# A fixed instruction order for the first batch's entry into a quantised attention and LoRA kernel

## The chip, the core and the metric

The kernel runs on one core of a Trainium2 chip. A core has a matrix engine (TensorE, "PE" in the profile, with its weight loads as "PEld"), a vector engine (VectorE, "DVE"), a scalar engine (ScalarE, "ACT"), a general engine (GpSimd, "POOL") and a queue engine (SyncE, "SP") that here only issues DMA transfers. Each engine executes its own instructions in the order in which they stand in its queue, and waits for the others by semaphores. The metric is the device time of one execution in microseconds (us), smaller being better.

## What is computed

Both layers work on two batches of 1024 tokens with 2048 features. The first is a product of two fake-quantised matrices, the second a feed-forward product with low-rank additions:

```python
def fake_quant(x, scale, zp):
    q = jnp.clip(jnp.round(x / s + z), 0.0, 255.0)
    return (q - z) * s

x = x + matmul(fake_quant(layernorm(x)), fake_quant(ctx))     # ctx: 2 x 2048 x 2048
h = layernorm(x)
x = x + (matmul(h, kernel) + bias                              # kernel: 2048 x 2048
         + low-rank terms of lora_A, lora_B chosen by gate, and of the shared pair)
```

`setup_inputs` gives x, ctx, four quantisation parameters, the gate (8 groups by 16 adapters), the kernel, the bias and the LoRA matrices, all float32.

## The kernel before

**Staging.** The two batches run one after the other. For each, the attention product comes first, then the normalisation for the second layer, then the feed-forward product as a seven-product scheme in two levels (`OUTER`, `INNER`, function `product`), in which TensorE is occupied nearly without a gap. During the last of the outer steps of the first batch, the second batch's ctx blocks and token tiles are already prepared. For the first batch nothing runs ahead, and the start of the program is this batch's entry.

**Tokens.** A batch has 8 token tiles of 128, in four groups of two. `prep_x` prepares one tile. VectorE takes statistics (`bn_stats`, four of 512 columns, L283; `norm_stats`, with the square root on ScalarE, L261), and seven small operations give scale and offset. ScalarE writes the quantised tile as uint8 (L295) and then, in two halves, as bf16 with 128 subtracted and with the row sum (L298). TensorE transposes each half in eight pieces of 128 (L303), and VectorE copies them out of PSUM (L304). `r_s` is the tile's row sum times a constant (L308). The uint8 halves and the bf16 halves of all tiles share the buffer `wk`.

**Context.** ctx is taken in four column blocks of 512, each in eight row blocks of 256 rows (512 KB). The ten buffers `lit` take the loads in turn. `quantise` turns one into bf16: ScalarE scales and clips at 0 into int16 (L314), VectorE clips at 255 and subtracts 128 (L317). Three buffers `q2b` stand between. `column_term` sums a finished block's columns: 16 small matmuls into four partial sums (L333), a copy (L343), an f32 matmul (L345) and a scaling on VectorE (L348).

**A pair.** `xattn_pair(b, n, g)` multiplies column block n with token group g: for both tiles ScalarE writes column term plus row sum into PSUM (L359), TensorE adds 16 matmuls (L361), then VectorE adds the result to `y` (L370) and takes statistics of it (L372). `ps_acc` has three accumulators for the pairs, used in turn; the small PSUM pool `ps_m` has two buffers for transposes and column sums.

**What sets the order.** The program is written for a scheduler that sorts each engine's instructions when the program is built: what was written earlier goes first when it is ready by the scheduler's own estimate, and what is ready may pass what is not. `tc.high_priority()` puts the writes of L359 ahead. `tc.issue_after(opened.ins)` puts VectorE's part of the tiles 4 to 7 behind the first pair's sum. The loads all go through SP's queue: token tile 0, two ctx blocks, tile 1, seven ctx blocks, tiles 2 and 3, then one ctx block for each one that is quantised, and tiles 4 to 7 behind the last quantisation of column block 0. `ahead[0]` limits how many loads are out at a time.

The order in which the first batch's entry is written is at the end of the function, at `for b in range(B)`: tile 0, eight quantisations with tile 1 among them, the column term, pair (0, 0), four quantisations, tiles 2 and 3, pair (0, 1), four quantisations, the second column term, pairs (1, 0) and (1, 1), and then the tiles and pairs of groups 2 and 3. Early in the program stand the gate values (L236 to L248): masks from the identity, a gate transfer on ScalarE's queue, products and sums on VectorE, and for each batch the matrix `gmat` (L694), which the LoRA steps use.

Of the kernel before, what the change touches and what calls it, by code (L numbers as in the profile page):

```python
# [10 lines left out]
F32 = mybir.dt.float32  # L11
# [55 lines left out]
def tile_quant_xattn_then_lora_ffn(  # L67
# [119 lines left out]


# [4 lines left out]
    ahead[0] = 2  # L193
    load_next()
    load_x(0, 1)
    ahead[0] = 9
    load_next()
    load_x(0, 2)
    load_x(0, 3)
# [11 lines left out]
    nc.gpsimd.memset(n_centre, -CENTRE)  # L211
    nc.vector.tensor_mul(s12, s1, s2)
# [16 lines left out]
    for tag in ("acc0", "acc1", "delta"):  # L229
# [3 lines left out]


    m_ad = const.tile([P, NL], F32, tag="m_ad", name="m_ad")
    nc.vector.tensor_reduce(m_ad, ident.rearrange("p (n r) -> p n r", r=RC), AX.X, ALU.add)  # L236
    m_rk = const.tile([P, RC], F32, tag="m_rk", name="m_rk")
    nc.vector.tensor_reduce(m_rk, ident.rearrange("p (n r) -> p r n", r=RC), AX.X, ALU.add)
    gate_b = const.tile([P, GB, NL], F32, tag="gate_b", name="gate_b")
    nc.scalar.dma_start(  # L240
        out=gate_b.rearrange("p b n -> p (b n)"),
        in_=gate.rearrange("b n -> (b n)").partition_broadcast(P),
    )
    gval = const.tile([P, GB], F32, tag="gval", name="gval")
    nc.vector.tensor_tensor(gate_b, gate_b, m_ad.unsqueeze(1).to_broadcast([P, GB, NL]), ALU.mult)
    for b in range(B):
        for i in range(2):
            nc.vector.tensor_reduce(  # L248
                gval[:, ds(b * GPB + i * 2, 2)], gate_b[:, b * GPB + i : (b + 1) * GPB : 2, :], AX.X, ALU.add
            )  # L250

    def norm_stats(stats, name):

        mv = small.tile([P, 2], F32, tag="mv", name=f"mv_{name}")
# [4 lines left out]
        nc.scalar.activation(sd, ve, AF.Sqrt)  # L261
        r0 = small.tile([P, 1], F32, tag="r0", name=f"r0_{name}")
# [14 lines left out]
    def prep_x(b, m, c1T, wk):  # L277

        nm = f"{b}_{m}"
# [4 lines left out]
        mean, rstd = norm_stats(st1[:, m], f"a{nm}")  # L284
# [5 lines left out]
        nc.vector.tensor_sub(o, z1, o)  # L290

# [3 lines left out]
        nc.scalar.activation(q8, ym, AF.Identity, bias=o, scale=k)  # L295
        rsum = small.tile([P, 2], F32, tag="rsum", name=f"rsum_{nm}")
        for h in range(2):
            nc.scalar.activation(  # L298
                qh[:, ds(h * H, H)], q8[:, ds(h * H, H)], AF.Identity, bias=n_centre, accum_out=rsum[:, h : h + 1]
            )  # L300
            pt = ps_m.tile([P, KH, P], BF16, tag="pm", name=f"pt_{nm}_{h}")
# [6 lines left out]
        nc.vector.tensor_mul(r_s[:, m : m + 1], r_c, d2)  # L308

    def quantise(c2, r):  # L310

        buf, t = next_loaded()
        qi = q2b.take()
        nc.scalar.activation(qi, t, AF.Relu, bias=z2, scale=inv2)  # L314
# [595 lines left out]
```

## Time and profile before

| what | value |
|---|---|
| time, median of 3 runs | 1128.51 us (1127.28 to 1128.93) |
| time of the profiled execution | 1128.61 us |
| span of the profile | 1126.8 us |
| TensorE busy | 1072.4 us (95%) |
| VectorE, ScalarE, GpSimd busy | 741.5, 261.1, 266.6 us |
| first attention matmul starts | 42.31 us |
| first matmul of the fifth pair starts | 83.87 us |

The profile is of one execution. "Busy" counts the time in which an engine executes something; a matmul's end is modelled, and matmuls overlap their weight loads. In the 40 slices each digit is the busy share of 28 us in tenths. A line of the timeline gives start, duration, engine, source line, operation, tiles and shapes; in brackets stands how long the engine was idle just before and what ended that.

### The profile page before, as it was taken

To read this page: it belongs to the slowest core of one execution; us is meant where nothing else is said; L and a number is where in the kernel's file an instruction comes from. 1 tells how busy PE (TensorE), PEld (TensorE's weight loads), DVE (VectorE), ACT (ScalarE), POOL (GpSimd) and SP (SyncE) were. 2 spreads that over 40 slices of the span, in tenths; PEclk is the share of its full clock that TensorE was granted. 3 is DMA by queue.
4 is the path that set the end of the run, shared out by engine and by line. 5 is a ranking of instruction groups with operands and counts; after the bars stand their busy time and mean duration, and the time that the engine had idled before them with its cause. 6 is when DMAs were issued, how large, how long until landed. Compare 5 with 4: busy or idle time off the path is not lost.

```text
span 1126.8 us, 10619 instructions
## 1 busy us (share of the span) xinstructions
PE 1072.4 (95%) x3926; PEld 489.3 (43%) x3926; DVE 741.5 (66%) x969; ACT 261.1 (23%) x342; POOL 266.6 (24%) x106
## 2 busy tenths in 40 slices
PE   1689899999999999999999999999999999999998
PEld 0244334554444444444444433455444444444443
DVE  4685547576696768568777654766668586865861
ACT  5875513320001010001375761232000000000000
POOL 0000000234253422525000000022535343243600
PEclk9999999999999999999999999999999999999999
DMA  8991935885789757489857094588668875749611
GB/s 307 391 244 35 282 124 217 298 322 205 246 285 377 266 181 264 141 301 355 285 184 228 1 277 154 182 301 314 244 215 293 295 255 181 256 145 322 213 38 56
DMA packets 120772, 261.35 MB, mean 232 GB/s; under 512 B 11920, under 2 KB 16144, under 8 KB 119568
## 3 DMA queue, kind: packets, MB, share of 16 engines
q1 hardware_dynamic: 99264, 218.65, 56.6%
q10 hardware_dynamic: 21456, 42.02, 10.5%
q8 instruction: 31, 0.51, 0.2%
q14 instruction: 21, 0.17, 0.0%
HBM read 224.99 MB, written 37.75 MB: 233 GB/s over the span
## 4 chain that ended last, share of the span: by engine, by line
PE 80%; DMA 7%; DVE 6%; ACT 4%; issue 1%; SPq 1%; ACTq 0%; DVEq 0%
PE fu L611 33%; PE fv L611 17%; PE pa L361 13%; PE fw L611 9%; DMA lit<-in_ctx_dram 4%; PE pl L483 3%; PE ptz L432 2%; DVE big L560 1%; PE pg_a L383 1%; DVE st L283 1%; PE pg_b L383 1%; ACT big L298 1%; ACT big L295 1%; DMA bd<-q2b 1%; DMA big<-in_w_dram 1%
## 5 line engine op out<-in xcount | busy, mean ns | idle before, releaser
L611 PE MATMUL fu<-big,lit 128*128 128x512 f32 x896 | 396.3, 594 | 2.4 <-DVE y L629 2.4
L560 POOL TENSOR_TENSOR lit<-lit,lit 128x1024 f32<-128x1024 f32 x56 | 165.2, 2957 | 539.4 <-PE pa L361 209.1
L611 PEld LDWEIGHTS fu<-big,lit 128*128 128x128 f32 x896 | 167.8, 190 | 208.2 <-issue 206.7
L361 PE MATMUL pa<-big,big 128*128 128x512 bf16 x1024 | 238.0, 382 | 11.9 <-ACT pa L359 10.6
L611 PE MATMUL fv<-big,lit 128*128 128x512 f32 x448 | 198.1, 594 | 0.0
L551 POOL TENSOR_TENSOR lit<-lit,lit 128x1024 f32<-128x1024 f32 x40 | 100.9, 2524 | 283.4 <-DMA lit<-zs 255.5
L560 DVE TENSOR_TENSOR big<-big,big 128x2048 f32<-128x2048 f32 x56 | 159.4, 2850 | 5.9 <-PE ptz L432 5.3
L361 PEld LDWEIGHTS <-big 128*128 128x128 bf16 x1024 | 97.0, 98 | 146.5 <-issue 44.3
L629 DVE TENSOR_TENSOR y<-y,fu 128x1024 f32<-128x1024 f32 (+1 forms) x98 | 113.7, 1194 | 67.2 <-PE fu L611 66.8
L611 PEld LDWEIGHTS fv<-big,lit 128*128 128x128 f32 x448 | 84.3, 190 | 105.0 <-issue 105.0
L629 DVE TENSOR_TENSOR y<-y,fv 128x1024 f32<-128x1024 f32 x48 | 56.8, 1218 | 91.1 <-PE fv L611 91.1
L478 ACT COPY pl<-bias 128x1024 f32<-128x1024 f32 x32 | 32.6, 1017 | 344.9 <-DVE y L493 327.1
L314 ACT ACTIVATE q2b<-lit,sc,inv 128x1024 int16<-128x1024 f32 x64 | 76.6, 1230 | 146.4 <-DMA lit<-in_ctx_dram 124.7
L551 DVE TENSOR_TENSOR big<-big,big 128x2048 f32<-128x2048 f32 x40 | 101.7, 2544 | 13.2 <-DMA big<-in_w_dram 13.2
L611 PE MATMUL fw<-big,lit 128*128 128x512 f32 x224 | 100.6, 596 | 0.1
L370 DVE SCALAR_TENSOR_TENSOR y<-pa,k_s,y 128x1024 f32<-128x1024 f32 x32 | 41.0, 1282 | 69.7 <-PE pa L361 69.7
L359 ACT ACTIVATE pa<-bp,r_s 128x512 f32<-128x512 f32 x64 | 42.8, 684 | 105.6 <-PE pa L361 60.5
L629 DVE TENSOR_TENSOR y<-y,fw 128x1024 f32<-128x1024 f32 x24 | 28.4, 1217 | 52.5 <-PE fw L611 52.5
L611 PEld LDWEIGHTS fw<-big,lit 128*128 128x128 f32 x224 | 41.3, 190 | 48.7 <-issue 48.2
L303 PE MATMUL pt<-ident_h,big 128*128 128x128 bf16 x256 | 20.3, 231 | 29.6 <-ACT big L298 29.4
L283 DVE BATCH_NORM_STATS2 st<-y 128x6 f32<-128x512 f32 x64 | 42.1, 680 | 2.9 <-DMA y<-in_x_dram 2.9
L317 DVE TENSOR_SCALAR big<-q2b 128x1024 bf16<-128x1024 int16 x64 | 27.6, 440 | 23.7 <-ACT q2b L314 20.5
(79 smaller groups left out, 609.9 us busy)
## 6 DMA issues: line engine op xcount, KB each, us to landing
big<-in_w_dram SPq DMA_DIRECT2D x96, 1024.0 KB
lit<-zs SPq DMA_DIRECT2D x88, 512.0 KB
lit<-in_ctx_dram SPq DMA_DIRECT2D x64, 512.0 KB
out_dram<-y ACTq DMA_DIRECT2D x30, 512.0 KB
zs<-lit ACTq DMA_DIRECT2D x24, 512.0 KB
y<-in_x_dram SPq DMA_DIRECT2D x8, 1024.0 KB
lit<-in_lora_a_dram SPq DMA_DIRECT2D x32, 256.0 KB
lit<-in_lora_bt_dram SPq DMA_DIRECT2D x32, 256.0 KB
```

The lines of the kernel that those rows point to most:

```text
L283: nc.vector.bn_stats(st1[:, m, n, :], ym[:, ds(n * NB, NB)])
L314: nc.scalar.activation(qi, t, AF.Relu, bias=z2, scale=inv2)
L317: nc.vector.tensor_scalar(c2[r // 4][:, ds(2 * (r % 4), 2), :], qi, QMAX, CENTRE, ALU.min, ALU.subtract)
L359: nc.scalar.activation(pa[:, j, :], colt[n], AF.Identity, bias=r_s[:, m : m + 1])
L361: nc.tensor.matmul(pa[:, j, :], c1T[g][:, k, ds(j * P, P)], c2[k // 8][:, k % 8, :], start=False, stop=(k == KT - 1), skip_group_check=True,)
L370: summed = nc.vector.scalar_tensor_tensor(yp, pa, s12, yp, ALU.mult, ALU.add)
L478: nc.scalar.copy(pl, self.bb.unsqueeze(1).to_broadcast([P, 2, NB]))
L483: nc.tensor.matmul(pl[:, i, ds(h * (NB // 2), NB // 2)], axT[rows, pr, ds(j * P, P)], self.bp[rows, ds(h * (NB // 2), NB // 2)], start=Fal ...
L551: line(eng.tensor_tensor(got[0], got[0], got[1], ALU.add if terms[1][2] > 0 else ALU.subtract))
L560: line(eng.tensor_tensor(out_t, at[p], at[q], op))
L611: nc.tensor.matmul(ps[:, m, :], at[:, k, ds(m * P, P)], bt[:, k, :], start=(opens and k == 0), stop=(ends and k == KQ - 1), skip_group_che ...
L629: line(nc.vector.tensor_tensor(yp, yp, chains[chain][:, js, :], ALU.add if sign > 0 else ALU.subtract))
```

## The change

The entry of the first batch, up to and with pair (0, 1), is written as one function, `begin_first`, and a context manager `in_order` ties every instruction of VectorE, ScalarE, TensorE and SyncE in it to the one before it on the same engine, so that the scheduler keeps the written order on these engines. To be able to interleave them, `prep_x`, `quantise` and `xattn_pair` become generators of steps. Each `next` runs one step and `fin` runs what is left. A tile's steps are: statistics and square root; the seven small operations; the uint8 tile; bf16 half 0; half 1; transposes and copy of half 0; of half 1; row sum.

In this order the second pair is (1, 0), the third (0, 1). All of column block 1 is loaded and quantised ahead of token tile 2, whose load stands behind 16 ctx blocks. Five of the sixteen quantisations (rows 1, 3, 7 of block 0, rows 2, 4 of block 1) use `quantise_v`, both steps on VectorE with a uint8 between. For these two blocks the column term is 16 whole matmuls into one PSUM buffer (`column_sum`), without the copy and the f32 matmul. Twelve matmuls on constants (`keep_busy`) stand among them. A square root of a constant is computed at the program's start. The gate values and their transfer move to the end of the entry, ahead of the second half of pair (0, 1). Four ctx blocks instead of two are loaded ahead of tile 1, and the limit of loads becomes 10.

```diff
+    last_of = {}
+    @contextmanager
+    def in_order(*engines):
+        traced = nc.cur_bb.bb.instructions
+        last = traced[-1]
+        yield
+        start = next(k for k in reversed(range(len(traced))) if traced[k] is last) + 1
+        for i in list(traced[start:]):
+            if i.engine in engines:
+                if i.engine in last_of:
+                    tc.add_manual_dep(
+                        i,
+                        last_of[i.engine].name,
+                        mybir.DependencyInfo(mybir.DependencyClass.NoSync, mybir.DependencyReason.DATA),
+                        reason="in_order",
+                    )
+                last_of[i.engine] = i
...
     load_x(0, 0)
-    ahead[0] = 2
+    ahead[0] = 4
     load_next()
     load_x(0, 1)
-    ahead[0] = 9
+    ahead[0] = 8
     load_next()
-    load_x(0, 2)
-    load_x(0, 3)
+    ahead[0] = 10
+    load_next()
...
+    warm = const.tile([P, 1], F32, tag="warm", name="warm")
+    nc.gpsimd.memset(warm, 1.0)
+    nc.scalar.activation(warm, warm, AF.Sqrt)
...
-    m_ad = const.tile([P, NL], F32, tag="m_ad", name="m_ad")
...
+    def gate_values():
+        m_ad = const.tile([P, NL], F32, tag="m_ad", name="m_ad")
+        nc.vector.tensor_reduce(m_ad, ident.rearrange("p (n r) -> p n r", r=RC), AX.X, ALU.add)
+        nc.vector.tensor_reduce(m_rk, ident.rearrange("p (n r) -> p r n", r=RC), AX.X, ALU.add)
+        gate_b = const.tile([P, GB, NL], F32, tag="gate_b", name="gate_b")
+        nc.scalar.dma_start(
+            out=gate_b.rearrange("p b n -> p (b n)"),
+            in_=gate.rearrange("b n -> (b n)").partition_broadcast(P),
+        )
...
+    def begin_stats(stats, name):
         mv = small.tile([P, 2], F32, tag="mv", name=f"mv_{name}")
         nc.vector.bn_aggr(mv, stats.rearrange("p n s -> p (n s)"))
         ve = small.tile([P, 1], F32, tag="ve", name=f"ve_{name}")
         nc.vector.tensor_scalar_add(ve, mv[:, 1:2], EPS)
         sd = small.tile([P, 1], F32, tag="sd", name=f"sd_{name}")
         nc.scalar.activation(sd, ve, AF.Sqrt)
+        return mv, ve, sd, name
+    def end_stats(mv, ve, sd, name):
...
+    def prep_x_steps(b, m, c1T, wk):
...
-        mean, rstd = norm_stats(st1[:, m], f"a{nm}")
+        begun = begin_stats(st1[:, m], f"a{nm}")
+        yield
+        mean, rstd = end_stats(*begun)
...
         nc.scalar.activation(q8, ym, AF.Identity, bias=o, scale=k)
+        yield
         rsum = small.tile([P, 2], F32, tag="rsum", name=f"rsum_{nm}")
         for h in range(2):
             nc.scalar.activation(
                 qh[:, ds(h * H, H)], q8[:, ds(h * H, H)], AF.Identity, bias=n_centre, accum_out=rsum[:, h : h + 1]
             )
+            yield
+        for h in range(2):
             pt = ps_m.tile([P, KH, P], BF16, tag="pm", name=f"pt_{nm}_{h}")
             for kt in range(KH):
                 nc.tensor.transpose(pt[:, kt, :], qh[:, ds(h * H + kt * P, P)], ident_h)
             nc.vector.tensor_copy(c1T[g][:, ds(h * KH, KH), tok], pt)
+            yield
...
+    def quantise_steps(c2, r):
         buf, t = next_loaded()
         qi = q2b.take()
         nc.scalar.activation(qi, t, AF.Relu, bias=z2, scale=inv2)
         lit.give(buf)
         load_next()
+        yield
         nc.vector.tensor_scalar(c2[r // 4][:, ds(2 * (r % 4), 2), :], qi, QMAX, CENTRE, ALU.min, ALU.subtract)
+        q2b.give(qi)
+    def quantise_v(c2, r):
+        buf, t = next_loaded()
+        qi = q2b.take()
+        q8 = flat(qi)[:, 0:NB].bitcast(U8).rearrange("p (k n) -> p k n", k=2)
+        nc.vector.tensor_scalar(q8, t, inv2, z2, ALU.mult, ALU.add)
+        lit.give(buf)
+        load_next()
+        nc.vector.tensor_scalar(c2[r // 4][:, ds(2 * (r % 4), 2), :], q8, CENTRE, None, ALU.subtract)
         q2b.give(qi)
...
+    def column_sum(pc, c2, ks):
+        for k in ks:
+            nc.tensor.matmul(pc, ones_h, c2[k // 8][:, k % 8, :], start=(k == 0), stop=(k == KT - 1))
+    def column_end(pc, n):
...
+    def xattn_steps(b, n, g, c1T, c2, apart=False):
         cols = ds(n * NB, NB)
         pairs.append((b, n, g))
         pa = ps_acc.tile([P, MG, NB], F32, tag=("acc0", "acc1", "delta")[len(pairs) % 3], name=f"pa_{b}_{n}_{g}")
-        for j in range(MG):
+        def first(j):
             m = g * MG + j
             with tc.high_priority():
                 nc.scalar.activation(pa[:, j, :], colt[n], AF.Identity, bias=r_s[:, m : m + 1])
+        if not apart:
+            for j in range(MG):
+                first(j)
+        for j in range(MG):
+            if apart:
+                first(j)
+            yield
             for k in range(KT):
+                if k == KT // 2:
+                    yield
...
+    def begin_first():
+        X = [prep_x_steps(0, m, c1T, wk) for m in range(4)]
+        def fin(gen):
+            for _ in gen:
+                pass
+        def q(n, r):
+            gen = quantise_steps(c2[n], r)
+            next(gen)
+            return gen
+        def keep_busy(n):
+            for i in range(n):
+                nc.tensor.matmul(idle[:, i % 2, :], ones_h, ones_h[:, 0:1].to_broadcast([P, NB]), start=True, stop=True)
+        idle = ps_acc.tile([P, 2, NB], F32, tag="delta", name="idle")
+        q0 = q(0, 0)
+        next(X[0])
+        fin(q0)
+        next(X[0])
+        quantise_v(c2[0], 1)
+        q2 = q(0, 2)
+        next(X[0])
+        fin(q2)
+        quantise_v(c2[0], 3)
+        next(X[0])
+        next(X[0])
+        pc = ps_m.tile([P, NB], F32, tag="pm", name="pc_first")
+        column_sum(pc, c2[0], range(8))
+        q4 = q(0, 4)
+        next(X[1])
+        q5 = q(0, 5)
+        load_x(0, 2)
+        load_x(0, 3)
+        next(X[1])
+        next(X[0])
+        fin(X[0])
+        keep_busy(8)
+        q6 = q(0, 6)
+        fin(q4)
+        fin(q5)
+        column_sum(pc, c2[0], range(8, 12))
+        keep_busy(4)
+        next(X[1])
+        quantise_v(c2[0], 7)
+        load_x(0, 4)
+        load_x(0, 5)
+        fin(q6)
+        column_sum(pc, c2[0], range(12, 16))
+        next(X[1])
+        column_end(pc, 0)
+        A = xattn_steps(0, 0, 0, c1T, c2[0], apart=True)
+        next(A)
+        next(X[1])
+        next(X[1])
+        next(A)
+        p0 = q(1, 0)
+        p1 = q(1, 1)
+        fin(p0)
+        fin(X[1])
+        next(A)
+        next(A)
+        quantise_v(c2[1], 2)
+        p3 = q(1, 3)
+        load_x(0, 6)
+        load_x(0, 7)
+        fin(p1)
+        quantise_v(c2[1], 4)
+        p5 = q(1, 5)
+        pc = ps_m.tile([P, NB], F32, tag="pm", name="pc_second")
+        next(A)
+        column_sum(pc, c2[1], range(0, 6))
+        next(X[2])
+        fin(p3)
+        p6 = q(1, 6)
+        fin(p5)
+        p7 = q(1, 7)
+        next(A)
+        fin(p6)
+        fin(p7)
+        column_sum(pc, c2[1], range(6, 16))
+        column_end(pc, 1)
+        next(X[2])
+        next(X[2])
+        A2 = xattn_steps(0, 1, 0, c1T, c2[1])
+        next(A2)
+        next(X[3])
+        next(X[2])
+        next(X[2])
+        next(X[3])
+        next(A2)
+        next(A2)
+        next(X[2])
+        fin(X[2])
+        next(A2)
+        next(A2)
+        fin(A)
+        next(X[3])
+        A3 = xattn_steps(0, 0, 1, c1T, c2[0], apart=True)
+        next(A3)
+        next(X[3])
+        next(X[3])
+        next(A2)
+        next(A3)
+        next(A3)
+        fin(A2)
+        next(X[3])
+        fin(X[3])
+        gate_values()
+        gate_matrix(0)
+        next(A3)
+        fin(A3)
+    def gate_matrix(b):
...
+    for b in range(B):
+        if b > 0:
+            gate_matrix(b)
         if b == 0:
             open_c2(0)
-            prep_x(0, 0, c1T, wk)
-            for r in range(NR):
-                quantise(c2[0], r)
-                if r == 3:
-                    prep_x(0, 1, c1T, wk)
-            for m in range(4, MT):
-                load_x(0, m)
             open_c2(1)
-            column_term(b, 0, c2[0])
-        opened = xattn_pair(b, 0, 0, c1T, c2[0])
-        if b == 0:
-            for r in range(4):
-                quantise(c2[1], r)
-            for m in (2, 3):
-                prep_x(b, m, c1T, wk)
-        xattn_pair(b, 0, 1, c1T, c2[0])
-        if b == 0:
-            for r in range(4, NR):
-                quantise(c2[1], r)
-            column_term(b, 1, c2[1])
-        for g in range(2):
-            xattn_pair(b, 1, g, c1T, c2[1])
+            with in_order(
+                mybir.EngineType.DVE, mybir.EngineType.Activation, mybir.EngineType.PE, mybir.EngineType.SP
+            ):
+                begin_first()
+            opened = summed[0]
+            xattn_pair(b, 1, 1, c1T, c2[1])
+        else:
+            opened = xattn_pair(b, 0, 0, c1T, c2[0])
+            xattn_pair(b, 0, 1, c1T, c2[0])
+            for g in range(2):
+                xattn_pair(b, 1, g, c1T, c2[1])
```

## The prediction

> **What bounds the kernel now.** I read the engine shares first, then the forty slices, then windows around the entry, then the timeline of the entry engine by engine.
>
> ```profile
> PE 1072.4 (95%) x3926; PEld 489.3 (43%) x3926; DVE 741.5 (66%) x969; ACT 261.1 (23%) x342; POOL 266.6 (24%) x106
> ...
> PE   1689899999999999999999999999999999999998
> ```
>
> TensorE (PE) is busy 95%, and what it lacks, 54.4 us, lies mostly in the first two slices of 28 us. The windows split it:
>
> ```profile
> 0.00:42.30 42.30, 10.77 (x56) 4.90 (x57) 22.34 (x71) 24.95 (x28) 1.25 (x10) 1.00 0.89 336
> 42.30:83.87 41.57, 35.79 (x203) 16.83 (x203) 30.16 (x97) 34.06 (x42) 0.00 (x0) 1.00 0.95 292
> 83.87:1126.80 1042.93, 1025.88 (x3671) 467.53 (x3668) 689.02 (x803) 202.12 (x274) 265.30 (x96) 1.00 0.65 225
> ```
>
> The columns after the stretch's length are the busy times of PE, PEld, DVE, ACT and POOL, then clock, DMA share and GB/s. Until the first attention matmul (42.31) PE is idle 31.5 us; up to the first matmul of the fifth pair (83.87) another 5.8; in the 1043 us after that 17.0, or 1.6%. So I count to the fifth pair only: what is gained there arrives at the end almost whole, since nothing but PE is near its limit later.
>
> ```profile
> 13.39 1.28 ACT L314 ACT_TABLE_LOAD   x1 [13.39 <-DMA lit<-in_ctx_dram]
> 15.94 1.28 ACT L261 ACT_TABLE_LOAD   x1
> 19.13 2.09 ACT L295 ACTIVATE big<-y,ox,kx 128x2048 uint8<-128x2048 f32 x1 [0.56 <-DVE ox L290]
> 42.31 5.53 PE L361 MATMUL pa<-big,big 128*128 128x512 bf16 x16 [1.91 <-ACT pa L359]
> 48.62 3.61 PE L361 MATMUL pa<-big,big 128*128 128x512 bf16 x16 [0.78 <-ACT pa L359]
> 52.27 1.28 DVE L370 SCALAR_TENSOR_TENSOR y<-pa,k_s,y 128x1024 f32<-128x1024 f32 x1 [1.02 <-PE pa L361]
> 70.31 2.09 ACT L295 ACTIVATE big<-y,ox,kx 128x2048 uint8<-128x2048 f32 x1 [2.04 <-DVE ox L290]
> ```
>
> To be seen: ScalarE (ACT) loads a table twice inside the entry; the first 16 matmuls take 5.53 us, the next 3.61 (0.226 each); the first pair's sum is at 52.27, and token tile 4, which may follow only that sum, is converted at 70.31.
>
> **The change, part by part.** I rework the entry by hand, each engine strictly in the new order, with row durations. On VectorE (DVE): four bn_stats 2.46 (19.01 to 21.47), aggregation and epsilon 0.42, the seven small operations after the square root 1.23, the second step of a quantisation 0.38, a transpose's copy 0.60, the column result 0.81, a pair's sum 1.28 and its two statistics 1.3. On ACT: quantisation 1.23, square root 0.20, a tile's conversion 2.08, its halves 1.13 each and 0.19 for the last read-out, an accumulator's start 0.67. On PE: 0.222 per matmul warm, 0.43 cold, eight transposes 0.56.
>
> Transfers: tile 0 lands at 10.2, the first ctx block at 13.4, both as now. Tile 1 now stands behind four blocks instead of two; at 390 GB/s (windows from 10 to 40) a 512 KB block is 1.35 us, so it lands at 19.7 instead of about 17.1. Tile 2 moves behind 16 blocks instead of 9 on SP's queue: 11.5 MB, 1.46 of them moved by 10 us, the rest at 0.39 MB/us, and 2.5 us for what is under way beside it: 38.2. It is wanted at 38.7, so it just fits; tiles 3 to 7 and the blocks among them land ahead of use.
>
> Five quantisations go from ACT to DVE, as f32 to uint8 and uint8 to bf16. No row shows either. The first lies between 0.81 (L428, 1024 f32 to f32, median) and 1.28 (L370); the second between 0.42 (L317, from int16) and 0.81. I take 0.81 and 0.55, L428 being nearest in form, so 1.36, with ends 1.23 and 2.09. [...]
>
> First stage, to the first attention matmul. Tile 0's statistics end at 13.2; ACT quantises block 0 from 13.4 to 14.6 without table loads (now both 1.28 us loads are on its way; one load is left, in the idle start) and takes the root by 14.8. DVE: 0.38, 1.23, 1.36, 0.38, 1.36, so 19.4. Tile 1's statistics run 19.7 to 22.7, the root to 23.0, the rest to 24.2; then tile 0's copies, which share one PSUM buffer because the column sum keeps the other, to 26.1, row sum 26.5, then three second steps and a DVE quantisation to 29.1. The last four column sums end at 30.0, the column result at 30.9, the accumulator start at 31.6: 10.7 us earlier than 42.31. The old column term (copy 0.69, two f32 matmuls 2.07) is gone with it. The twelve idle matmuls fill 26 to 29, where PE waits anyway: nothing, as long as DVE holds the last rows until 29.1, else at most 12 x 0.43 = 5.2.
>
> Second stage. Pair one: eight matmuls, tile 1's transposes, eight, a 0.4 wait for the second start, eight, six column sums, eight: done at 41.2 (now 52.2). Here the order bites. DVE reads tile 2's statistics (38.7 to 41.6); behind that root ACT holds the last two quantisations, to 44.3; the rows are ready at 44.8. PE idles 3.7 us, then ten column sums cold 3.9, to 48.7. Column result 49.5, tile 2's seven operations 50.8, its conversion on ACT 52.9, and only behind it the second pair's start, 53.6. PE idles 4.9. Then eight cold and eight warm to 58.9, tile 2's transposes, eight, eight, and sixteen of the third pair to 67.3, tile 3's transposes, a wait of 1.8 for its row sum and start, sixteen to 73.8, and the fourth pair to 80.9 (now 83.3).
>
> The clock: after a gap of 2.15 us (before 67.50) 21 matmuls took 4.69, full rate; after one of 7.83 (before 33.54) 16 transposes took 2.17 against 1.06 warm. The gaps of 3.7 and 4.9 lie between. The weight loads from 42.3 kept a step of 0.43 until 46.1, so warming took 3.8 us, and I take gaps that long as cooling: (10 + 8) x 0.21 = 3.8 us, with 0 as the other end. [...]
>
> Third stage. The fifth pair needs tile 4, whose statistics stand behind the first pair's sum on DVE. That sum moves from 52.27 to 61.1, since the order puts it behind tile 2's copies. DVE then has the sum and statistics of pairs one and two to 66.3, two of tile 4's four statistics, tile 3's copies and row sum to 69.5, gate values 1.8, the other two and the root to 73.2, and the small operations around pair three's sum, to 75.5. ACT converts to 77.6, halves to 80.0; transposes, copy and start: 82.9, behind pair four's end by 2.0, of which 1.1 are transposes. Now that matmul is at 83.87, but by then 0.5 us of tile 5's transposes are done too. Net -0.5.
>
> The gate load moves from 1.66 on ACT's queue to about 64. It now took up to 8.7 us (SP waits for it until 10.38). DVE wants it at 70.2; behind it wait the gate products, pair three's sum and half of tile 4's statistics. Landing between 1 and 9 us after issue costs 0 to 2.8; I take 0, since 6 us cover it. The load limit of 10 for 9 issues each load a place earlier, but ten buffers turn either way: 0. The extra memset is on POOL, idle there.
>
> Sum: -10.7 at the entry, +10.2 given back by 82.9: the profiled execution of 1128.61 (span 1126.8 and 1.8 around it, 0.1 above the median) becomes 1128.1, by the median 1128.0.
>
> **Rivals.** (a) The gaps do not cool PE: everything PE-paced up to the fifth pair moves 3.8 up, the late tile 4 included, since its DVE work hangs on the pairs' sums: 1124.2. For it: the 2.15 us gap stayed warm. Against it: 42.31 to 46.1 was slow.
>
> (b) Slower, by DVE's conversions alone: at 2.09 each instead of 1.36 three of them lengthen the chain to 31.6 and two that to the second column sum: 5 x 0.73 = 3.7, hence 1131.7. It decides from 0.55 us a conversion on (2.8 in all, past the 0.5 gained and the measurable bound). For it: in my schedule DVE has hardly a gap from 13 to 29. Against it: L428 runs 1024 f32 in 0.81.
>
> (c) The gate load lands late: DVE stands 2.8 us ahead of tile 4: 1130.8.
>
> (d) The entry keeps its gain: tile 4 is not late and the DMA is ahead of my pace, so that only the idle PE stretches are given back: 1 to 2 us on (a), 1122.5.
>
> **How the numbers follow.** A time within 0.2%, 2.3 us, can't be told from no change. No change to speak of 0.33; (a) 0.18 and (d) 0.13 give faster 0.31; (b) 0.22 and (c) 0.14 give slower 0.36, a little more than faster because a strict order turns each late input into a stop of everything behind it. The range goes from near (a), 1123.5, to 1133.0, (b) with a part of (c); the likeliest case alone spans 1126.3 to 1130.6.
>
> **What would show it.** Right: first attention matmul near 31.6; one table load, ahead of 10 us; PE gaps of about 4 and 5 us between 41 and 54, with matmuls near 0.43 after them; pair one's sum near 61; fifth pair near 83. Wrong: matmuls at 0.22 behind the gaps (a); conversions over 1.9 us a pair of steps (b); a DVE wait for the gate transfer (c); tile 2's statistics waiting for its transfer beyond 40, which no case prices and which would add its own length.

## The result, and the profile after

The changed kernel took 1135.57 us (median of 9 runs, 1132.75 to 1140.58) against 1128.49 for the kernel before (9 runs, 1127.28 to 1130.36). The ratio is 1.0065, with a 95% interval of 1.0048 to 1.0083: slower by 7.1 us, and 2.6 us beyond the upper end of the predicted range. Its profiled execution took 1140.58 us, 5.0 above its own median, so what is read from that trace is held below against that of ahead9, a kernel whose time is not to be told from this one's. In what follows a "stand" is a stretch in which an engine is idle. The pairs are numbered as they run: in the changed kernel one is (0, 0), two (1, 0), three (0, 1), four (1, 1), and the fifth is the first of token tiles 4 and 5. A tile is "converted" when ScalarE starts to write it as uint8.

The engine shares and two rows of the slices, of the changed kernel:

```profile
PE 1080.1 (95%) x3934; PEld 497.5 (44%) x3934; DVE 745.1 (65%) x972; ACT 255.2 (22%) x337; POOL 263.9 (23%) x107
...
PE   4778999999999999999999799989999999999998
...
PEclk9898999999999999999999899999999999999999
```

TensorE (PE) is still busy 95% of the span. The first two slices rose from 1 and 6 to 4 and 7 as intended, but the next two fell from 8 and 9 to 7 and 8, and two slices fell in the middle: 626 to 655 us (a 7), where the second batch passes the place that the change rewrote for the first, and 740 to 769 (an 8), where its attention passes into the second layer. The clock row shows three slices below 9: the second, the fourth, and that of 626 to 655 us. Before had none, though its records of the clock begin only at 46.22 us, so that the slow first 16 matmuls (5.53 us for 3.61) left no mark in that row.

The windows, cut at the same two events as before (first attention matmul, fifth pair's first matmul); columns as before:

```profile
0.00:32.07 32.07, 13.90 (x58) 6.05 (x59) 17.76 (x49) 16.09 (x19) 1.29 (x11) 0.95 0.86 322
32.07:86.86 54.79, 40.21 (x216) 19.28 (x216) 42.99 (x121) 35.94 (x48) 0.00 (x0) 0.89 0.90 297
86.86:1138.80 1051.94, 1026.01 (x3660) 472.22 (x3659) 684.30 (x804) 203.17 (x272) 262.62 (x96) 0.99 0.65 223
```

The first attention matmul came 10.2 us earlier (32.07 for 42.31). The stretch to the fifth pair grew by 13.2 us (54.79 for 41.57), so that this pair begins 3.0 us later than before. The rest grew by another 9.0 (1051.94 for 1042.93). The 12.0 us of this execution are thus 3.0 up to the fifth pair and 9.0 behind it, where the prediction had nothing.

The timeline of the changed kernel, all engines, in the order of time; the last bracket is the idle time ahead of the instruction and what ended it:

```profile
1.66 1.28 ACT L235 ACT_TABLE_LOAD   x1 [1.66 <-PEq L1088]
32.07 1.89 PE L443 MATMUL pa<-big,big 128*128 128x512 bf16 x8 [1.18 <-ACT pa L431]
35.55 0.81 DVE L372 TENSOR_SCALAR q2b<-lit,inv,sc 128x1024 uint8<-128x1024 f32 x1
36.39 0.69 DVE L375 TENSOR_SCALAR big<-q2b 128x1024 bf16<-128x1024 uint8 x1
42.12 2.08 PE L409 MATMUL pc_second<-big,ones_h 128*128 128x512 bf16 x8 [0.30 <-DVE big L364]
44.27 0.43 DVE L364 TENSOR_SCALAR big<-q2b 128x1024 bf16<-128x1024 int16 x1 [0.71 <-ACT q2b L360]
44.75 0.59 PE L409 MATMUL pc_second<-big,ones_h 128*128 128x512 bf16 x2 [0.54 <-DVE big L364]
50.96 5.22 PE L443 MATMUL pa<-big,big 128*128 128x512 bf16 x16 [5.62 <-ACT pa L431]
56.66 1.29 DVE L345 COPY big<-pt 128x1024 bf16<-128x1024 bf16 x2 [4.22 <-PE pt L344]
58.13 1.27 DVE L453 SCALAR_TENSOR_TENSOR y<-pa,k_s,y 128x1024 f32<-128x1024 f32 x1
68.22 12.03 PE L443 MATMUL pa<-big,big 128*128 128x512 bf16 x48 [3.35 <-ACT pa L431]
73.38 1.28 DVE L453 SCALAR_TENSOR_TENSOR y<-pa,k_s,y 128x1024 f32<-128x1024 f32 x1 [1.31 <-PE pa L443]
76.08 2.09 ACT L333 ACTIVATE big<-y,ox,kx 128x2048 uint8<-128x2048 f32 x1 [1.05 <-DVE ox L327]
80.08 1.17 PE L344 MATMUL pt<-ident_h,big 128*128 128x128 bf16 x16
83.94 0.62 PE L344 MATMUL pt<-ident_h,big 128*128 128x128 bf16 x8 [2.68 <-ACT big L337]
85.07 1.03 PE L344 MATMUL pt<-ident_h,big 128*128 128x128 bf16 x8 [0.51 <-ACT big L337]
86.86 16.39 PE L443 MATMUL pa<-big,big 128*128 128x512 bf16 x64 [0.76 <-ACT pa L431]
```

Three things are to be seen. VectorE (DVE) stands 4.22 us for tile 2's transposes while pair one's products, complete since 41.8, wait behind that stand for their sum (58.13; before 52.27); tile 4's preparation may follow only that sum, and its conversion is at 76.08 (before 70.31). Then all 32 transposes of tiles 4 and 5 stand on PE ahead of the fifth pair, and 64 matmuls follow in one block. And the matmuls behind the stands of 5.62 and 3.35 us run slow: 16 in 5.22 us, where the trace before has 16 in 3.61; the granted clock is 0.50 from 47.4 to 54.2 and from 67.9 to 71.3. Before, the same 32 transposes stood in groups of 13, 11 and 8, with pair four's second half and the fifth pair's first matmuls between:

```profile
78.86 0.89 PE L303 MATMUL pt<-ident_h,big 128*128 128x128 bf16 x13
79.80 3.61 PE L361 MATMUL pa<-big,big 128*128 128x512 bf16 x16
83.25 0.78 PE L303 MATMUL pt<-ident_h,big 128*128 128x128 bf16 x11
83.87 1.67 PE L361 MATMUL pa<-big,big 128*128 128x512 bf16 x7
85.39 0.61 PE L303 MATMUL pt<-ident_h,big 128*128 128x128 bf16 x8
```

The second batch, whose program the change seemed not to touch. Three groups on PE of the kernel before, then of the changed kernel with the DVE row that goes with them:

```profile
600.69 17.15 PE L361 MATMUL pa<-big,big 128*128 128x512 bf16 x78
618.46 0.62 PE L303 MATMUL pt<-ident_h,big 128*128 128x128 bf16 x8 [0.62 <-ACT big L298]
...
620.16 4.48 PE L361 MATMUL pa<-big,big 128*128 128x512 bf16 x20
```

```profile
605.62 21.32 PE L443 MATMUL pa<-big,big 128*128 128x512 bf16 x98
...
616.02 0.69 DVE L318 BATCH_NORM_STATS2 st<-y 128x6 f32<-128x512 f32 x1 [3.28 <-DMA y<-in_x_dram]
...
626.77 1.06 PE L344 MATMUL pt<-ident_h,big 128*128 128x128 bf16 x16
633.75 2.17 PE L344 MATMUL pt<-ident_h,big 128*128 128x128 bf16 x16 [5.92 <-ACT big L337]
...
746.07 1.06 PE L514 MATMUL ptz<-ident,big 128*128 128x128 f32 x8 [2.84 <-DVE big L510]
```

Before put tile 4's first transposes and 20 more matmuls of the pairs at hand in turn; after does 98 matmuls, 16 transposes, and then PE stands 5.92 us for tile 5. The same block order as in the first batch, though the second batch's pairs go through the plain `xattn_pair`. The last line is the other place, in the slice from 740 us: PE stands 2.84 us for VectorE, which itself waits for a square root that ScalarE runs only at 744.03, behind two DMA issues.

### The profile page after: what moved, and what is told of

Same layout as the page of the kernel before. It is cut to its first block, busy times and chain, and to the rows that moved or that the text cites. A ratio compares the mean times of both kernels' runs of the same rounds, so it can differ in the third digit from the quotient of the medians.

```text
span 1138.8 us, 10629 instructions
## 1 busy us (share of the span) xinstructions
PE 1080.1 (95%) x3934; PEld 497.5 (44%) x3934; DVE 745.1 (65%) x972; ACT 255.2 (22%) x337; POOL 263.9 (23%) x107
## 4 chain that ended last, share of the span: by engine, by line
PE 81%; DMA 10%; DVE 5%; ACT 2%; SPq 1%; issue 1%; ACTq 0%; DVEq 0%
PE fu L693 33%; PE fv L693 16%; PE pa L443 13%; PE fw L693 9%; PE pl L565 3%; DMA lit<-in_ctx_dram 2%; DMA y<-in_x_dram 2%; PE px L530 2%; PE ptz L514 2%; DMA bd<-q2b 1%; DMA zs<-lit 1%; DVE st L318 1%; DMA lit<-in_lora_a_dram 1%; PE pg_a L465 1%; ACT big L337 1%
## 5 line engine op out<-in xcount | busy, mean ns | idle before, releaser
L642 POOL TENSOR_TENSOR lit<-lit,lit 128x1024 f32<-128x1024 f32 x56 | 164.2, 2940 | 516.0 <-DMA bd<-q2b 211.6
L633 POOL TENSOR_TENSOR lit<-lit,lit 128x1024 f32<-128x1024 f32 x40 | 99.2, 2482 | 321.7 <-DMA lit<-zs 274.5
L443 PEld LDWEIGHTS <-big 128*128 128x128 bf16 x1024 | 100.0, 100 | 145.7 <-issue 40.4
L360 ACT ACTIVATE q2b<-lit,sc,inv 128x1024 int16<-128x1024 f32 x59 | 70.4, 1231 | 166.6 <-DMA lit<-in_ctx_dram 129.0
L514 PE MATMUL ptz<-ident,big 128*128 128x128 f32 x256 | 36.9, 287 | 6.5 <-DVE big L510 3.9
L575 DVE TENSOR_TENSOR y<-pl,y 128x512 f32<-128x512 f32 x64 | 41.0, 681 | 1.1
```

The source lines that it names most:

```text
L443: nc.tensor.matmul(pa[:, j, :], c1T[g][:, k, ds(j * P, P)], c2[k // 8][:, k % 8, :], start=False, stop=(k == KT - 1), skip_group_check=True,)
L514: nc.tensor.transpose(pt[:, k, :], t[:, ds((4 * u + k) * P, P)], ident)
L575: line(nc.vector.tensor_add(yb, pl[:, i, :], yb))
L633: line(eng.tensor_tensor(got[0], got[0], got[1], ALU.add if terms[1][2] > 0 else ALU.subtract))
L642: line(eng.tensor_tensor(out_t, at[p], at[q], op))
```

## The experiments

Theories put to the test: (one) the rewritten `xattn_steps` writes both accumulator starts of a pair ahead of its matmuls, also outside the entry, and the scheduler then keeps pairs in blocks; (two) PE's stands in the entry and the half clock behind them; (three) the order of a tile's halves and transposes; (four) the tenth load ahead; and, added after the first four runs, (five) tile 4 released late because pair one's sum is written late. Each median stands beside its ratio to the kernel before, measured in the same runs; the profile is of one execution.

**The written order of the pairs, undone (pair_old).**

```diff
-        for _ in xattn_steps(b, n, g, c1T, c2):
+        for _ in xattn_steps(b, n, g, c1T, c2, apart=True):
```

> The changed kernel, with the pairs outside the entry in the order in which the kernel before writes them: accumulator start of the first token tile, its 16 matmuls, start of the second, its 16 matmuls (the change writes both starts first). Theory one, that this order is the loss: in the trace of after, tile 4's and tile 5's transposes stand ahead of all 64 matmuls of pairs five and six in both batches, TensorE is 3.0 us late at the fifth pair of batch 0 and stands still 5.92 us in batch 1; the delay is 4.4 us at the end of batch 0's FFN and 12 at the end of the span. It expects the 7.6 us of batch 1 back and part of the 4.4: 1126 to 1130 us, with transposes and matmuls in groups of fewer than 32 in batch 1 and no stand of over 2 us there. Theory two, that the entry's own stands (5.6 us ahead of the second pair, 3.35 ahead of the third's second half) are carried to the end: 1134 to 1137, as after.

Measured: 1137.82 us, ratio 1.0085 (1.0072 to 1.0098). No gain; theory one alone fails. Transposes and matmuls do take turns again, but (timeline of this kernel, ScalarE and PE):

```profile
82.61 2.09 ACT L333 ACTIVATE big<-y,ox,kx 128x2048 uint8<-128x2048 f32 x1 [2.23 <-DVE ox L327]
84.61 1.28 ACT L431 ACTIVATE pa<-bp,r_s 128x512 f32<-128x512 f32 x2
...
85.33 0.59 PE L443 MATMUL pa<-big,big 128*128 128x512 bf16 x1 [4.27 <-ACT pa L431]
```

Tile 4 is as late as in after (converted at 75.88), there is no other work left that could be put between, and the fifth pair's start on ScalarE (ACT) now waits behind tile 5's conversion: PE stands 4.27 us, and behind that 16 transposes take 2.16 us (from 87.11), where 16 took 1.06 at 64.95.

**That order alone, in the kernel before (pair_only).**

```diff
         for j in range(MG):
             ...
                 nc.scalar.activation(pa[:, j, :], colt[n], AF.Identity, bias=r_s[:, m : m + 1])
+        for j in range(MG):
             for k in range(KT):
```

> The kernel before with one edit alone: a pair's two accumulator starts are written ahead of its matmuls. Theory one (this order is the loss): batch 1 comes out in blocks as in after, and the time is 6 to 12 us over the kernel before, 1134 to 1140. Theory two (the entry's stands are the loss): nothing changes, 1127.5 to 1129.5.

Measured: 1137.60 us, ratio 1.0084 (1.0071 to 1.0097): one moved line costs 9 us, in a kernel with the old entry. PE of this kernel, from the third pair on:

```profile
70.69 15.66 PE L362 MATMUL pa<-big,big 128*128 128x512 bf16 x63 [3.75 <-ACT pa L359]
86.19 1.06 PE L303 MATMUL pt<-ident_h,big 128*128 128x128 bf16 x16
88.33 0.61 PE L303 MATMUL pt<-ident_h,big 128*128 128x128 bf16 x8 [1.08 <-DVE big L304]
90.11 1.20 PE L303 MATMUL pt<-ident_h,big 128*128 128x128 bf16 x16 [1.18 <-DVE big L304]
92.95 0.58 PE L362 MATMUL pa<-big,big 128*128 128x512 bf16 x1 [1.64 <-ACT pa L359]
```

All transposes wait for the end of four pairs, though tile 4 was ready long before, and then stand in one row, each half a copy behind the other. So the order is a cause, but not the only one. Where it costs was not as expected: of the 7.0 us by which its profiled execution is longer than that of before, 6.9 are there by the first sum of batch 1, hardly any behind it (0.1). That execution took 1135.63 us, 2.0 less than the median, and where these 2.0 lie is not shown.

**A tile's steps in the old order as well (both_old).** Outside the entry `prep_x` goes back to half, transposes, half, transposes.

```diff
+            if not late:
+                turn(h)
             yield
-        for h in range(2):
-            pt = ps_m.tile([P, KH, P], BF16, tag="pm", name=f"pt_{nm}_{h}")
...
+        for h in range(2 if late else 0):
+            turn(h)
             yield
```

`turn(h)` holds the eight transposes and the copy as they were; `prep_x` passes `late=False`, the entry `late=True`.

> As the kernel with the pairs written in the old order, and outside the entry also a token tile's steps as before: first half converted, its eight transposes, second half converted, its eight transposes (the change writes both conversions first). Theory three, that this order costs by itself because the first half's transposes wait for the second conversion: 1 to 4 us less than the kernel with the old pairs alone. Theory one: within 1 us of it, since a scheduler that ranks by readiness places the transposes by when their half is ready.

Measured: 1137.15 us, 1.0075 (1.0063 to 1.0087), within 1 us of pair_old: theory three finds no support.

**Nine loads ahead for ten (ahead9).**

```diff
-    ahead[0] = 10
+    ahead[0] = 9
```

> The changed kernel with at most 9 loads ahead in the entry in place of 10. Theory four, that the tenth load crowds x or the gate's load and is part of the loss: 1130 to 1134 us. Theories one and two: as after, 1134.5 to 1136.5.

Measured: 1134.84 us, 1.0061 (1.0047 to 1.0075), not to be told from after: theory four falls.

**Pair one's sum ahead of tile 2's transposes (sum1).**

```diff
         next(A2)
         next(A2)
+        fin(A)
         next(X[2])
         fin(X[2])
         next(A2)
         next(A2)
-        fin(A)
```

> The changed kernel with one step moved: pair one's sum and its statistics are written ahead of tile 2's transposes instead of behind them. In the trace of after, DVE stands 4.22 us (52.44 to 56.66) for those transposes while pair one's products have been ready since 41.8, the sum starts at 58.13 (52.27 before), and the preparation of tiles 4 to 7 is issued only after that sum: tile 4's offset is ready at 75.9 (70.1 before), and the fifth pair begins at 86.9 (83.9 before). Theory five, that this late release is the loss of batch 0: sum at 52.4, tile 4's offset at about 71 to 72, fifth pair at about 83, and 3 to 4.5 us off the time: 1131 to 1132.5. Theory two, that the loss is the stands of TensorE ahead of the second and third pair and the half clock behind them: those stay, and the time with them, 1134.5 to 1136.5.

Measured: 1134.07 us, 1.0046 (1.0034 to 1.0058): 1.5 us off, not 3 to 4.5. The first half of the expectation holds, the second does not (timeline, DVE, ACT, PE):

```profile
52.89 1.28 DVE L453 SCALAR_TENSOR_TENSOR y<-pa,k_s,y 128x1024 f32<-128x1024 f32 x1
...
69.69 4.08 ACT L333 ACTIVATE big<-y,ox,kx 128x2048 uint8<-128x2048 f32 x2 [0.92 <-DVE ox L327]
...
80.26 1.06 PE L344 MATMUL pt<-ident_h,big 128*128 128x128 bf16 x16
...
87.02 3.17 PE L443 MATMUL pa<-big,big 128*128 128x512 bf16 x8 [1.64 <-ACT pa L431]
```

The sum comes at 52.89, tile 4 is converted from 69.69, 6.4 us earlier than in after, with tile 5 right behind it. Yet the transposes of tile 4 still begin at 80.26, behind pair four, and 24 more stand ahead of the fifth pair, which is not earlier at all (87.02). Here the block order is the limit; in pair_old it was tile 4. The two limits lie one behind the other, and either repair alone meets the other.

**The second pair's starts ahead of tile 2's conversion (start1).**

```diff
-        next(X[2])
-        next(X[2])
         A2 = xattn_steps(0, 1, 0, c1T, c2[1])
         next(A2)
+        next(X[2])
+        next(X[2])
```

> The changed kernel with one step moved: the accumulator starts of the second pair are written ahead of tile 2's offset and conversion, so that TensorE's stand ahead of that pair falls from 5.62 us to about 2. Theory two (stands and half clock): 2 to 4 us off, 1131.5 to 1133.5. Theory five (release of tile 4 by pair one's sum): tile 2's conversion comes 1.3 us later, the sum with it, and the time is the same or up to 1.5 us more, 1135.5 to 1137.

Measured: 1134.30 us, 1.0044 (1.0029 to 1.0059). The stand falls from 5.62 to 2.51 us and the fifth pair begins at 83.56, 3.3 earlier than in after. The median is 1.3 us less than after's; the profiled execution took 1129.81, 4.5 below that median, so its trace does not show where the rest of the 3.3 goes. Tile 4 did not come later, as theory five had it, since the sum follows the second pair's faster progress (54.9).

**Both moves (both1), and both with the old order of the pairs (both_po).** The edits are those of sum1 and start1; both_po adds that of pair_old.

> Both moves together. Theory five: 1131 to 1133, as the sum alone. Theory two: as the starts alone. If both carry a part, the gains add: 1128 to 1131.

> Both moves, and the pairs outside the entry in the old written order (start, 16 matmuls, start, 16 matmuls). In the changed kernel that order gave 1137.8 against 1135.6, as the first start of the fifth pair stood behind tile 5's quantisation. If tile 4 comes earlier now, TensorE still has the fourth pair to do when tile 4 is ready and the old order has room to put transposes between matmuls: 1126 to 1130. If tile 5's quantisation is still ahead of the start: 1130 to 1133.

Measured: both1 1129.91 us, 1.0012 (0.9999 to 1.0025), not to be told from the kernel before; both_po 1124.56 us, 0.9965 (0.9952 to 0.9979), faster than both kernels. ACT and PE of both_po, and the clock of all that follows:

```profile
69.64 2.09 ACT L333 ACTIVATE big<-y,ox,kx 128x2048 uint8<-128x2048 f32 x1 [1.18 <-DVE ox L327]
...
76.50 1.28 ACT L431 ACTIVATE pa<-bp,r_s 128x512 f32<-128x512 f32 x2
...
78.00 1.25 PE L443 MATMUL pa<-big,big 128*128 128x512 bf16 x5 [1.14 <-DVE big L345]
```

```profile
53.90:1122.30 1068.40, 1047.64 (x3807) 478.57 (x3805) 712.97 (x883) 222.02 (x301) 265.52 (x96) 1.00 0.67 227
```

The fifth pair begins at 78.00, 5.9 us ahead of the kernel before and 8.9 ahead of after, and the clock stays full from 53.9 to the end.

**Each move with the old order (sum_po, start_po).**

> Of the version at 1124.6 us (both moves, old written order of the pairs) the sum's move and the old order alone. The three edits together took 11 us off; the sum's move alone took 1.5, the starts' alone 1.3, the old order alone added 2.3. If the release of tile 4 by pair one's sum is what makes the old order pay: 1125 to 1128, and tile 5's quantisation stands no longer ahead of the fifth pair's start. If the second pair's early starts are: 1134 to 1138.

> The starts' move and the old order alone. If the release of tile 4 by pair one's sum makes the old order pay: the sum comes only some 3 us earlier here (54.9 against 58.1 in the kernel with this move alone), 1131 to 1136. If the early starts do: 1125 to 1128.

Measured: sum_po 1126.79 us, 0.9989 (0.9973 to 1.0004); start_po 1129.27 us, 1.0006 (0.9995 to 1.0017). The early sum makes the old order pay (11.0 us less than pair_old), as expected. The early starts do so nearly as well (8.5 us less), between the two expectations: there tile 4 is converted at 72.43 and the fifth pair begins at 79.38. What both have in common is that tile 4 is converted 3.5 to 5.2 us earlier than in pair_old. So what the old order is worth depends on the rest of the entry: it saves 7.3 us with the sum moved, 5.0 with the starts moved, 5.4 with both, and costs 2.3 with neither.

**Idle matmuls in the two stands (warm).**

```diff
         column_sum(pc, c2[1], range(6, 16))
+        keep_busy(22)
...
         fin(X[3])
+        idle = ps_acc.tile([P, 2, NB], F32, tag="acc1", name="idle2")
+        keep_busy(14)
         gate_values()
```

> The changed kernel with 22 idle matmuls in TensorE's stand of 5.62 us ahead of the second pair and 14 in that of 3.35 us ahead of the third pair's second half; nothing else is touched. In after the clock is at half from 47.4 to 54.2 and from 67.9 to 71.3. Theory two, that this half clock is a main part of the loss: full clock through both, and 2.5 to 4 us off, 1131.5 to 1133. Theory five, that the fifth pair waits for the preparation of tile 4 and not for TensorE: pair four ends earlier, pair five hardly, 1133.5 to 1136.

Measured: 1131.60 us, 1.0027 (1.0013 to 1.0041): 4.0 us off, by nothing but work that PE throws away. Its timeline and window:

```profile
45.76 4.95 PE L790 MATMUL idle<-ones_h 128*128 128x512 bf16 x22
52.21 3.61 PE L443 MATMUL pa<-big,big 128*128 128x512 bf16 x16 [1.50 <-ACT pa L431]
```

```profile
28.30:82.90 54.60, 47.13 (x265) 22.73 (x263) 42.61 (x114) 34.63 (x44) 0.00 (x0) 1.00 0.99 325
```

The second pair's 16 matmuls begin 1.25 us later than in after and take 3.61 us for 5.22. The fifth pair comes 1.7 earlier (85.18), not "hardly", and at batch 1's first sum the gain is 4.0. The 1.7 reach it through VectorE: tile 4's offset stands there behind pair three's sum, which waits for PE (73.38 in after, 71.69 here). So half clock in the entry was about half of the loss: theory two holds as a part. Where the other 2.3 of the 4.0 are gained, between the fifth pair and batch 1, is not shown.

**All together, the gate's reductions moved out (best).** both_po with 10 idle matmuls ahead of the second pair, and `gate_values()` and `gate_matrix(0)` written just ahead of the pairs of token tiles 6 and 7.

> The version at 1124.6 us with two edits more: the gate's reductions (2.0 us of DVE, between tile 4's statistics and its offset) moved out of the entry to just ahead of the fourth pair of token tiles, and 10 idle matmuls ahead of the second pair. If DVE's queue is what holds tile 4 still: its offset 1 to 2 us earlier, 1122 to 1124. If TensorE's own work is the bound by now: 1124 to 1126.

Measured: 1125.85 us, 0.9973 (0.9960 to 0.9987). Not better than both_po, whose interval overlaps. The fifth pair begins at 77.92, as in both_po (78.00): the gate's reductions on DVE did not hold it.

**One table of the profiled executions.** Order: whether pairs outside the entry run in blocks or in turn with transposes. Pair five: its first matmul. Sum: the first pair's sum of batch 1, so all of batch 0. Rest: span less that sum. Stand: PE's longest in batch 1 ahead of tiles 4 and 5, and x: DVE's wait for a tile of x there. Times in us. One execution need not stand for its kernel: those of after and both1 took 5.0 and 5.3 us more than their medians, those of start1 and pair_only 4.5 and 2.0 less.

| kernel | order | tile 4 converted | pair five | sum | rest | stand | x | ratio |
|---|---|---|---|---|---|---|---|---|
| before | turns | 70.3 | 83.9 | 602.0 | 524.8 | 0.6 | 0 | 1 |
| after | blocks | 76.1 | 86.9 | 606.6 | 532.2 | 5.92 | 3.28 | 1.0065 |
| pair_only | blocks | 71.2 | 93.0 | 608.8 | 525.0 | 2.74 | 0 | 1.0084 |
| ahead9 | blocks | 76.8 | 87.6 | 605.8 | 526.3 | 2.56 | 0 | 1.0061 |
| sum1 | blocks | 69.7 | 87.0 | 603.6 | 528.7 | 3.50 | 0.84 | 1.0046 |
| start1 | blocks | 72.8 | 83.6 | 599.4 | 528.6 | 5.57 | 2.92 | 1.0044 |
| both1 | blocks | 69.0 | 85.0 | 603.7 | 529.7 | 4.94 | 2.29 | 1.0012 |
| warm | blocks | 74.4 | 85.2 | 602.6 | 526.0 | 3.19 | 0.54 | 1.0027 |
| pair_old | turns | 75.9 | 85.3 | 608.9 | 528.7 | 3.09 | 2.36 | 1.0085 |
| both_old | turns | 76.7 | 86.1 | 610.6 | 525.5 | 0.96 | 0.24 | 1.0075 |
| start_po | turns | 72.4 | 79.4 | 602.0 | 527.2 | 1.72 | 1.00 | 1.0006 |
| sum_po | turns | 70.7 | 80.9 | 599.6 | 525.2 | 0.98 | 0.25 | 0.9989 |
| both_po | turns | 69.6 | 78.0 | 597.5 | 524.8 | 0.74 | 0 | 0.9965 |
| best | turns | 69.4 | 77.9 | 596.2 | 528.2 | 2.46 | 1.74 | 0.9973 |

The stand in batch 1 is the wait for x plus a constant: 2.6 to 2.7 us where pairs run in blocks, 0.7 where they take turns. The block order thus costs some 1.9 us of standing there, on top of the wait for x; how much of it reaches the end is open, as pair_only, which stands 2.74 us, has a rest only 0.1 us above that of before. Behind the sum after's profiled execution is 7.4 us longer than before, and that of ahead9, in the same order, 1.5. A part of this difference is the wait for x (3.28 against 0); another is the stand of 2.84 us at 743, where ahead9's is 0.68. Behind PE's stand ahead of tiles 4 and 5 (the column of the table) 16 transposes took 2.17 us in after (clock 0.50 from 631.1 to 641.3) and in both1, against 1.06 for the 16 ahead of it; in before, pair_only, start_po and best the eight behind it took 0.62, as at full clock. Of the median loss of 7.1 us, 4.6 are in batch 0 by after's trace (3.8 by that of ahead9); the remaining 2.5 lie among the 0.1 to 7.4 by which the "rest" of the block kernels exceeds that of before. This split is an estimate, from one execution each. What makes x land early or late in batch 1 was not tried and stays open.

## Why the prediction was wrong, point by point

**The entry's front part was right.** One table load at 1.66; first attention matmul at 32.07 (31.6 forecast). The DVE conversions took 0.81 and 0.69, 1.50 for the pair against 1.36 taken and inside the bounds. For the second step the 0.55 taken between the rows of 0.42 (L317) and 0.81 (L428) was too low by 0.14.

**The second stage was right in kind.** The first stand (3.7 forecast, ahead of ten column sums) did not come. The last two quantisations did follow tile 2's root (41.77), and the last row was ready at 44.7, as forecast (44.8); but each column sum waits for its own row only, so eight of the ten ran from 42.12, after 0.30 us, and two at 44.75, after 0.54. The second did, with 5.62 us for 4.9. Pair one's sum was at 58.13 for 61.1, tile 4's conversion began at 76.08 and ended at 78.2 for 77.6.

**The cold cost came out right in part by luck, and ended too early.** The 3.8 us of "(10 + 8) x 0.21" assumed two gaps and nothing behind them; of the 18 cold matmuls the ten column sums were to follow the gap that did not come. In its place a wait that was forecast at 1.8 and as harmless, that for the third pair's second half, became 3.35, with the clock at half behind it. Measured: the second pair's first half at 1.6 us too much (5.22 for 3.61), half clock again from 67.9 to 71.3 behind the 3.35 us stand and from 85.0 to 91.8 behind the transposes. The windows of these two stretches have a granted clock of 0.50. Filling the two stands (5.62 and 3.35) brought 4.0 us, so the size was near 3.8 for another pair of stands than the forecast one; the third stretch at half, mostly behind the fifth pair's beginning, lay outside what was counted.

**The step that failed first is the third stage: "transposes, copy and start: 82.9, behind pair four's end by 2.0".** Halves were ready at 80.5, as forecast at 80.0, but the fifth pair began at 86.86, 4.0 us later than the forecast. I put tile 4's transposes and the start as in the trace before. In the changed kernel all 16 transposes follow pair four, their copies (81.84 and 83.63) share DVE with pair four's sum and statistics, and tile 5's 16 transposes stand ahead of the pair, as tile 5's second half does on ScalarE ahead of the pair's starts (84.92). The cause is in the diff as printed: outside the entry `apart` is false and both starts precede the matmuls. I described the two functions as turned into generators and priced the rewrite of the pairs outside the entry at nothing. pair_only shows what this costs in the kernel before: 9 us. In the changed kernel it is not to be had back alone (pair_old), since tile 4 was late as well.

**The second is the frame: "what is gained there arrives at the end almost whole".** It was meant for a gain and used as the reason to stop looking at the fifth pair. Of the profiled execution's 12.0 us, 9.0 lie behind that point, and both changed functions are called there too.

**The costs put at nothing.** The gate's load cost nothing, as forecast: no DVE wait for it is in the trace, and best without it gains nothing to be told. The tenth load cost nothing (ahead9).

**The rivals.** (a), uncooled gaps, is refuted by the clock; (b) by 1.50 us a conversion; (c) by the missing wait; (d) by tile 4 at 76.08. Slower had the largest of the three chances (0.36), but through (b) and (c), which are both refuted; that the time moved that way for another reason is luck. The true mechanism was in none of the rivals. That two limits lay one behind the other (late tile 4, blocks on PE) was foreseen by no case: of the three edits in both_po each alone gave at most 1.5 us, or lost 2.3; together they gave 11.0.

## What to carry to other kernels

When a helper is turned into a generator for one place, compare the order in which it writes instructions in every other place: where a scheduler ranks by written order, one moved start can turn interleaved work into blocks. In an order fixed by hand, write a finished result's use ahead of any instruction that waits for another engine, above all when later work is released by it. And where a repair brings nothing, test it together with the next suspect before it is dropped: two waits in a row hide each other.

## What the runs showed of the hardware

In the traces of before and after, the records of PE's granted clock begin at 46.22 and 20.11 us and change only at whole multiples of 3.41 us from there. Cut into stretches of that length, nine at full clock had PE busy 35% or less (counted from its instructions), and behind each of them the next was at half (two of the nine at the program's end). All others at full clock had PE busy 57% or more, and behind each of those the next was full. Of the stretches at half in after that end within the program, seven had PE busy 81% or more and were followed by full clock; four were followed by half again, with 0, 22, 75 and 87%. What sets the one of 87% apart is not shown. The windows of two stretches in warm, and of the 2.15 us stand in before that the prediction had used:

```profile
209.20:212.60 3.40, 1.40 (x7) 0.83 (x7) 1.58 (x2) 1.45 (x3) 3.32 (x2) 1.00 1.04 364
212.60:216.00 3.40, 3.40 (x11) 2.27 (x10) 3.40 (x4) 1.17 (x2) 3.40 (x2) 0.50 0.60 228
```

```profile
63.30:66.70 3.40, 2.05 (x8) 0.82 (x7) 3.40 (x9) 2.04 (x2) 0.00 (x0) 1.00 1.07 311
66.70:70.10 3.40, 2.60 (x13) 1.18 (x13) 3.40 (x13) 1.50 (x3) 0.00 (x0) 1.00 1.03 247
```

Behind 2.00 us idle within one stretch (1.40 of 3.40 us busy) the clock was 0.50; behind the stand of 2.15 us, which fell across two (2.05 and 2.60 busy), it stayed 1.00 and 21 matmuls took 4.69 us. Transposes took longer at half clock too: in after 16 took 1.06 us at full (626.77) and 2.17 at half (633.75).
